# A four-layer graph network on one core: the last layer's order kept in SBUF, its first tile prepared inside the third layer

## The chip, the cores and the metric

The kernel runs on one core of one Trainium2 chip. A core has a matrix engine (PE, with its weight loads shown apart as PEld), VectorE (DVE), ScalarE (ACT), GpSimd (POOL) and a queue engine for transfers (SP). The metric is device time in microseconds (us) of one execution. Engines run their instructions in the order in which they were built into the program, and wait for one another by semaphores.

## The reference, cut to what matters

Eight batches of 2048 nodes with 64 features pass through four layers, each of the form `x = x + layer(relu(layernorm(x)), adj)`. The third and the fourth layer matter here. The third does three message steps with the adjacency matrix, and the fourth is a graph attention:

```python
def _L2_gnn_ref(causal_vars, adj_matrix, W1, b1, W2, b2):   # third layer
    for _ in range(MAX_STEPS):            # 3
        effects = einsum('nm,bmd->bnd', adj_matrix, v)
        h = concatenate([v, effects], axis=-1)
        h = relu(einsum('bnk,dk->bnd', h, W1) + b1)
        v = einsum('bnk,dk->bnd', h, W2) + b2

def _L3_gnn_ref(x, adj, weight, a, bias): # fourth layer
    adj = adj.at[diag_indices(N)].set(1.0)
    h = einsum('bni,io->bno', x, weight)
    e_src = h @ a[:D, 0]
    e_dst = h @ a[D:, 0]
    e = leaky_relu(e_src[:, :, None] + e_dst[:, None, :], negative_slope=0.2)
    e = adj[None, :, :] * e
    attention = softmax(e, axis=-1)
    return einsum('bij,bjd->bid', attention, h) + bias
```

Where adj is 0 the score is 0, not minus infinity, so every node still gives its share with weight exp(0 - maximum). The sum over all nodes of h is therefore used as a base, and only the neighbours' terms differ from it.

## The kernel before, in words

A flag computed at the start picks a short path for sparse graphs; it is the one that runs. The nodes are ordered by the number of their neighbours and cut into 16 tiles of 128. The first tile has the nodes with the most neighbours. For tiles 1 to 15 the kernel makes lists of neighbours, with fixed lengths (`NEAR`: 20, 14, 12, 10, ... 3). The first tile is treated densely.

**The lists** are made by `neighbours` (line 1506) inside the third layer's first steps. It ranks the nodes, writes the order to a small DRAM buffer (`order3`), and then, for tiles 1 to 15, gathers 128 rows of adj at a time with an indirect transfer on POOL (line 1530) into one of two row buffers in slot q4, masks them and takes eight column numbers at a time with VectorE's maximum instruction.

**The third layer** (`layer2`, line 1431) runs three steps of `adj_product`. A step goes over four chunks of 512 nodes. A chunk takes 16 adjacency tiles; ScalarE casts each (line 325), and PE does eight products of 128x128 by 128x512 per tile (line 166). Between two chunks PE makes the messages of the next step, and VectorE adds a bias to them (line 1453). A hook called after every adjacency tile (`after`, line 1461) advances the making of the lists. In the third step each finished chunk goes through `Scores.chunk`: layer norm, projection with the fourth layer's weights, and a store of 528 values per node (features and two sets of scores) to the DRAM tensor `f_rows` (lines 1982 and 1983). There `sq` and `hn` are two buffers in slot q3, and `total`, the sum over all nodes, lies in the first quarter of `sq`.

**The fourth layer** is `layer3_near` (line 1562) with the class `Near` (line 1998). Two generators are interleaved:

- `first_tile` (line 2143) loads the order back from DRAM (line 2022), gathers the first tile's adj rows (line 2149), sets the diagonal and counts (line 2156), transposes them with PE in four groups (line 2164) and copies each group to SBUF (line 2165). It fetches its own feature rows (`mine`), computes a bound on the scores (`highest`) and spreads two vectors of scores over all partitions (lines 2185 and 2186). Then, for each of 16 node tiles, ScalarE does 16 exponentials (lines 2201 and 2202), VectorE a maximum and a mask (lines 2205 and 2206), and PE one product for `plain` and eight for `first`. Each node tile has four stops at which the other generator may go on.
- `others` (line 2080) treats the list tiles in the order `TILES = [15, 13, 11, 1, 10, 2, 9, 3, 8, 4, 7, 5, 6, 12, 14]` (line 2002). `block` (line 2064) gathers one feature row per node and list place: 1 + NEAR[t] indirect transfers of 128 rows each (line 2048), put by POOL into a ring of 36 places. VectorE makes the weights (lines 2093 to 2110) and the products (lines 2119 and 2138), and PE adds them up in `acc` with the identity. The result of a tile goes back to DRAM by another indirect transfer (`put_back`, line 2059). Tiles 15, 13, 11 and 1 fill the ring's 36 places exactly; tile 10 starts over at place 0.

`layer3_near` first takes one step of each, then twelve steps of `first_tile`, and then alternates. After both, `result` loads the rows back and adds them to x. The instructions of each engine are then arranged by a scheduler, so their order is not simply that of the code; tiles in named slots (q0 to q5) are shared by stages, and a write waits for the last reader of its place.

Of the kernel before, what the change touches and what calls it, by code (L numbers as in the profile page):

```python
# [7 lines left out]
F = mybir.dt.float32  # L8
# [3 lines left out]
I32 = mybir.dt.int32  # L12
# [115 lines left out]
class Kernel:  # L128
# [8 lines left out]
    def __init__(self, tc, ctx, a):  # L137
        self.tc, self.nc, self.a = tc, tc.nc, a
        self.flip = 0
        self.short = False  # L140
        self.consts = ctx.enter_context(tc.tile_pool(reuse_waits="tile", name="consts", bufs=1))

        dram = ctx.enter_context(tc.tile_pool(reuse_waits="tile", name="dram", bufs=1, space=bass.MemoryType.DRAM))
        self.xs = [
            [a["xT"][:, :, c * CW : (c + 1) * CW].rearrange("q p n -> p q n") for c in range(NC)]
        ]


        self.h_rows = dram.tile([N, ROW], F, name="h_rows")
        self.g_rows = dram.tile([N, NB * D], F, name="g_rows")  # L150
        self.order3 = dram.tile([P, 2, NT], I32, name="order3")
# [1279 lines left out]
    def layer2(self, slots, k2):  # L1431
# [4 lines left out]
        with (  # L1436
# [19 lines left out]
            if self.short:  # L1456
                near = self.neighbours(k, lambda: ps2.tile([P, CW], F, name="p2"), slots)
            last = Scores(self, slots, k, w, ps2) if self.short else None
            turn = [0]

            def after(ch, m, at):
                turn[0] += 1
                if turn[0] % 2:
                    next(near, None)

            for step in range(3):
                if step == 2:
# [3 lines left out]
                if step > 0:  # L1471
                    for t in range(NT):
                        self.split(u_n, t, u(t))

                def first(ch, out, step=step):
                    s = slice(ch * CW, (ch + 1) * CW)
# [29 lines left out]
    def neighbours(self, k, bank, slots):  # L1506
# [1 line left out]


        nc = self.nc  # L1510
        order = k.tile([P, 2, NT], I32, name="order")
        w = Parts(slots.tile([P, 2 * N], F, name="sort", tag="q4"))
        rank = self.ranks(w, bank, 1, NEAR[1])
        yield
        self.by_rank(w, bank, rank, order)
        nc.sync.dma_start(self.order3, order)
        yield
        own = k.tile([P, NT], F, name="own1")
        nc.vector.tensor_scalar(own, order[:, 1], 1.0, None, op0=OP.add)
        rows = slots.tile([P, 2, N], F, name="near_rows", tag="q4")  # L1520
        line = slots.tile([P, 2, N], F, name="line", tag="q5")
# [6 lines left out]
        for t in range(1, NT):  # L1528
# [33 lines left out]
    def layer3_near(self, slots):  # L1562

        tc = self.tc
        with (
            tc.tile_pool(reuse_waits="tile", name="att", bufs=1) as w,  # L1570
            tc.tile_pool(reuse_waits="tile", name="att_ps", bufs=1, space=PSUM) as ps,
        ):
            near = Near(self, slots, w, ps)
            first = near.first_tile()
            others = near.others()
            next(first)
            next(others)
# [346 lines left out]
class Scores:  # L1924
# [73 lines left out]
class Near:  # L1998
# [5 lines left out]
    def __init__(self, kern, slots, w, ps):  # L2004
        self.kern, self.nc, self.w, self.ps = kern, kern.nc, w, ps
        nc = self.nc
        *_, self.y, self.total, self.rows = kern.last_slots(slots)
        self.turn = 0
        x = slots.tile([P, 2, NP, CW], F, name="x_end", tag="q2")
        more = w.tile([P, 2, NP, CW], F, name="x_more")  # L2010
        self.x = [x[:, 0], x[:, 1], more[:, 0], more[:, 1]]
        two = slots.tile([P, 2, N], F, name="first_row", tag="q0")
        self.row, self.whole = two[:, 0], two[:, 1].bitcast(I32)
# [129 lines left out]
    def first_tile(self):  # L2143

        nc, w, ps, kern = self.nc, self.w, self.ps, self.kern
        ident = kern.ident

        row, whole, at, on_all = self.row, self.whole, self.first_at, self.on_all
        nc.gpsimd.indirect_dma_start(
            row, None, kern.a["adj"], bass.IndirectOffsetOnAxis(ap=self.order[:, 1, :1], axis=0)  # L2150
        )
        nc.gpsimd.iota(whole, pattern=[[1, N]], base=0, channel_multiplier=0)  # L2152
        own = w.tile([P, 1], F, name="own")
        nc.vector.tensor_copy(own, self.order[:, 1, :1])
        few = w.tile([P, 1], F, name="few")
        nc.vector.scalar_tensor_tensor(
            row, whole, own, row, op0=OP.is_equal, op1=OP.max, accum_out=few
        )
        nc.vector.tensor_scalar(few, few, -1.0, float(N), op0=OP.mult, op1=OP.add)
        for g in range(NT // 4):  # L2160
            pt = ps.tile([P, 4, P], F, name="pt", bufs=2)
            for i in range(4):
                c = 4 * g + i
                nc.tensor.transpose(pt[:, i], row[:, c * P : (c + 1) * P], ident)
            nc.scalar.copy(at[:, 4 * g : 4 * g + 4], pt)
# [85 lines left out]
def kernel(tc, a):  # L2251
    with ExitStack() as ctx:
        kern = Kernel(tc, ctx, a)
        with (
# [4 lines left out]

            kern.scores = flags.tile([P, NT, 2 * NB], F, name="scores")  # L2260
            kern.near = flags.tile([P, FIRST[NT]], F, name="near")
            with tc.tile_pool(reuse_waits="tile", name="check", bufs=1) as slots.pool:
                flag = kern.start(flags, slots)
            long = tc.nc.values_load(flag, min_val=0, max_val=1)
# [86 lines left out]
```

## Time and profile before

| | us |
|---|---|
| median of 3 runs | 2163.15 |
| lowest and highest | 2158.54, 2169.57 |
| the profiled execution | 2161.53 |
| its span | 2159.8 |
| PE busy | 1945.0 (90%) |
| DVE busy | 1133.9 (53%) |
| ACT busy | 712.2 (33%) |
| POOL busy | 706.0 (33%) |

The span runs from the first to the last instruction of the profiled execution, and what lies around it makes up the rest of its own time. The fourth layer's gathers begin at 1883.32 us of the span, the last rows are stored by POOL at 2122.93, and the closing transfers end the span. A share of busy time is an average over stages, so each stage has to be read for itself. In a line of the order in time the columns are start, duration, engine, line, operation, output and inputs with their forms, and count; in square brackets stands the idle time before and what ended it. Line numbers are those of the kernel before.

### The profile page before, as it was taken

The numbers are of one execution on the slowest core, as the hardware profiler recorded it, in microseconds if no ns is written. First come the engines' busy times: TensorE is split into PE (matmuls) and PEld (weight loads), VectorE is DVE, ScalarE is ACT, GpSimd is POOL, SyncE is SP. The second block draws the span as 40 slices with busy tenths as digits, with TensorE's granted clock in tenths as the row PEclk, the third lists the DMA queues.
The fourth block names the chain that finished last, engine by engine and source line by source line (L and its number), as shares of the span: only waits on it lengthen the run. The fifth ranks groups of instructions, "written<-read, shape, count | busy, mean of one in ns | idle before, by whom it ended". The sixth has DMA issues, their size and how long they took to land. (4 is left out here: it accounts for less than half of the span.)

```text
span 2159.8 us, 21301 instructions
## 1 busy us (share of the span) xinstructions
PE 1945.0 (90%) x7466; PEld 1163.0 (54%) x7466; DVE 1133.9 (53%) x1956; ACT 712.2 (33%) x1343; POOL 706.0 (33%) x595
## 2 busy tenths in 40 slices
PE   5879999978879999999999998899999999669885
PEld 1425766642237774353453543677777666445433
DVE  7877677736661123425434255698703222248774
ACT  6412555534543440020110201324335333248400
POOL 0000467754310005707447166011000000177870
PEclk8868999987769999999999999999999999879997
DMA  8230333441024460050230500556444444375665
GB/s 318 82 109 6 103 104 116 134 166 39 40 80 126 123 175 31 5 151 1 73 83 0 122 1 28 169 176 223 167 125 129 135 149 147 132 221 166 177 184 183
DMA packets 108796, 253.64 MB, mean 117 GB/s; under 512 B 20912, under 2 KB 21056, under 8 KB 101376
## 3 DMA queue, kind: packets, MB, share of 16 engines
q1 hardware_dynamic: 89264, 181.45, 27.0%
q0 software_dynamic: 17104, 66.47, 10.1%
q10 hardware_dynamic: 2304, 4.20, 0.5%
q8 instruction: 62, 1.02, 0.2%
q14 instruction: 62, 0.51, 0.1%
HBM read 218.30 MB, written 33.78 MB: 117 GB/s over the span
## 5 line engine op out<-in xcount | busy, mean ns | idle before, releaser
L325 ACT CAST adj<-adj_t 128x512 fp32r<-128x512 f32 x384 | 237.4, 619 | 687.2 <-PE pp L166 354.7
L1408 POOL TENSOR_TENSOR acc<-acc,y 128x512 f32<-128x512 f32 x224 | 277.2, 1269 | 449.2 <-DVE y L1403 449.2
L166 PE MATMUL pp<-adj,hi 128*128 128x512 f32 x1280 | 365.6, 405 | 0.1
L166 PE MATMUL pk<-q,w 128*128 128x512 f32 (+1 forms) x1024 | 358.2, 611 | 4.3 <-ACT q L1376 3.0
L166 PE MATMUL pp<-adj,lo 128*128 128x512 f32 x1280 | 358.7, 400 | 0.0
L166 PEld LDWEIGHTS pp<-adj,hi 128*128 128x128 f32 x1280 | 242.1, 191 | 72.4 <-issue 16.0
L166 PEld LDWEIGHTS pp<-adj,lo 128*128 128x128 f32 x1280 | 244.0, 191 | 56.5
L166 PEld LDWEIGHTS pk<-q,w 128*128 128x128 f32 (+1 forms) x1024 | 136.5, 188 | 214.1 <-issue 167.3
L1403 DVE SCALAR_TENSOR_TENSOR y<-pk,bias,q 128x512 f32<-128x512 f32 x224 | 157.7, 746 | 142.0 <-PE pk L166 135.7
L166 PE MATMUL acc<-q,ident 128*128 128x512 f32 x416 | 202.9, 614 | 26.4 <-DVE q L2138 16.5
L2048 POOL DMA_INDIRECT ring<-f_rows,near x121 | 139.7, 1154 | 67.0 <-issue 28.0
L166 PEld LDWEIGHTS acc<-q,ident 128*128 128x128 f32 x416 | 76.7, 194 | 102.4 <-issue 47.2
L2152 POOL IOTA q<- 128x2048 int32 x1 | 1.8, 1834 | 316.5 <-PE p L166 316.5
L166 PE MATMUL pp<-adj,x_ind_hi 128*128 128x512 f32 x256 | 94.7, 486 | 2.2 <-DVE q L738 1.9
L1840 POOL TENSOR_TENSOR q<-q,beta 128x512 f32<-128x512 f32 x57 | 67.9, 1193 | 54.6 <-DVE beta L1816 30.8
L1403 DVE SCALAR_TENSOR_TENSOR acc<-pk,bias,q 128x512 f32<-128x512 f32 x32 | 22.6, 747 | 119.9 <-PE pk L166 119.9
L166 PE MATMUL bank<-std,from_rows 32*128 32x512 f32 x128 | 46.7, 894 | 41.9 <-DVE std L273 33.8
L2119 DVE TENSOR_TENSOR q<-ring,e 128x1024 f32<-128x1024 f32 x58 | 70.1, 1219 | 8.9 <-PE acc L166 8.8
L166 PE MATMUL pp<-adj,x_ind_lo 128*128 128x512 f32 x256 | 71.7, 399 | 0.0
L1530 POOL DMA_INDIRECT q<-in_adj_dram,order x15 | 19.0, 1270 | 160.3 <-DVE top L1544 133.5
L166 PEld LDWEIGHTS pp<-adj,x_ind_hi 128*128 128x128 f32 x256 | 48.5, 189 | 38.9 <-issue 23.7
L1495 DVE SCALAR_TENSOR_TENSOR q<-p,cols,q 128x512 f32<-128x512 f32 x16 | 12.0, 751 | 108.4 <-PE p L166 107.5
(411 smaller groups left out, 2768.4 us busy)
## 6 DMA issues: line engine op xcount, KB each, us to landing
adj_t<-in_adjT_dram SPq DMA_DIRECT2D x128, 512.0 KB, 4.0
adj_t<-in_adjT_dram SPq DMA_DIRECT2D x128, 256.0 KB, 3.3
rows<-in_adj_dram SPq DMA_DIRECT2D x16, 1024.0 KB, 5.6
q<-x SPq DMA_DIRECT2D x10, 1024.0 KB, 4.9
x<-q SPq DMA_DIRECT2D x9, 1024.0 KB, 3.9
q<-in_embT_dram SPq DMA_DIRECT2D x8, 1024.0 KB, 11.5
x_ch<-in_xT_dram SPq DMA_DIRECT2D x4, 1024.0 KB, 6.3
h_rows<-q SPq DMA_DIRECT2D x16, 256.0 KB, 3.6
```

Source lines behind the costliest of these rows:

```text
L166: self.nc.tensor.matmul(out, lhsT, rhs, start=start, stop=stop)
L325: nc.scalar.copy(moving, at[:, i])
L1403: nc.vector.scalar_tensor_tensor(y, pks[b, half], bias[:, b : b + 1], emb[:, b], op0=OP.add, op1=OP.mult,)
L1408: nc.gpsimd.tensor_add(acc, acc, y)
L1495: nc.vector.scalar_tensor_tensor(x[:, q], p2, self.col("b2"), x[:, q], op0=OP.add, op1=OP.add)
L1530: nc.gpsimd.indirect_dma_start(row, None, self.a["adj"], bass.IndirectOffsetOnAxis(ap=order[:, 1, t : t + 1], axis=0),)
L1840: self.nc.gpsimd.tensor_tensor(x, x, by.unsqueeze(2).to_broadcast([P, NB, D]), op=OP.mult)
L2048: self.nc.gpsimd.indirect_dma_start(to, None, self.kern.f_rows[:], bass.IndirectOffsetOnAxis(ap=index, axis=0))
L2119: nc.vector.tensor_tensor(y.rearrange("n i (b f) -> n i b f", b=NB), block[:, i : i + 2, : NB * D].rearrange("n i (b f) -> n i b f", b=NB) ...
L2152: nc.gpsimd.iota(whole, pattern=[[1, N]], base=0, channel_multiplier=0)
```

## The change

- The order stays in an SBUF tile (`kern.order`) that lives through the third and fourth layers; its store to DRAM and its load are gone.
- A new generator, `first_rows`, gathers the first tile's adj rows, sets the diagonal, counts, transposes and copies them. It is advanced by the hook of the third layer's third step, one part per adjacency tile. It reuses the row buffer and the line of numbers of `neighbours`, and writes the turned rows into the half of slot q3 that belonged to `hn`. The iota and the copy of the own number in the fourth layer are gone.
- `hn` now lies in the place of `sq`, so `total` lies in `hn`. The ring of products (`y`) moves from the old `hn` to slot q1, where the turned rows had been.
- In `first_tile`, `mine` is fetched ahead of the first stop, so it comes ahead of the lists' first gathers. Twenty-four steps of `first_tile` instead of twelve are taken before the two generators alternate.

```diff
@@ layer2: @@
+            ahead = iter(())
             turn = [0]

             def after(ch, m, at):
                 turn[0] += 1
                 if turn[0] % 2:
                     next(near, None)
+                next(ahead, None)
...
+                if step == 2 and self.short:
+                    ahead = self.first_rows(slots, lambda: ps2.tile([P, CW], F, name="p2"))
@@ neighbours: @@
-        order = k.tile([P, 2, NT], I32, name="order")
+        order = self.order
...
-        nc.sync.dma_start(self.order3, order)
         yield
-        own = k.tile([P, NT], F, name="own1")
+        own = self.own_next = k.tile([P, NT], F, name="own1")
@@ new: @@
+    def first_rows(self, slots, bank):
+        nc = self.nc
+        row = slots.tile([P, 2, N], F, name="near_rows", tag="q4")[:, 0]
+        line = slots.tile([P, 2, N], F, name="line", tag="q5")[:, 0]
+        *_, at, _ = self.last_slots(slots)
+        nc.gpsimd.indirect_dma_start(
+            row, None, self.a["adj"], bass.IndirectOffsetOnAxis(ap=self.order[:, 1, :1], axis=0)
+        )
+        yield
+        few = self.few
+        nc.vector.scalar_tensor_tensor(
+            row, line, self.own_next[:, :1], row, op0=OP.is_equal, op1=OP.max, accum_out=few
+        )
+        nc.vector.tensor_scalar(few, few, -1.0, float(N), op0=OP.mult, op1=OP.add)
+        yield
+        for g in range(NT // 4):
+            pt = bank()
+            for i in range(4):
+                c = 4 * g + i
+                nc.tensor.transpose(
+                    pt[:, i * P : (i + 1) * P], row[:, c * P : (c + 1) * P], self.ident
+                )
+            nc.scalar.copy(at[:, 4 * g : 4 * g + 4].rearrange("p t n -> p (t n)"), pt)
+            yield
@@ last_slots: @@
-        return one[:, 0], one[:, 1], two[:, 0], two[:, 1], two[:, 0, 0], rows
+        at = two[:, 1].rearrange("p q n -> p (q n)").rearrange("p (t n) -> p t n", t=NT)
+        return one[:, 0], one[:, 1], two[:, 0], two[:, 0, 0], at, rows
@@ layer3_near: @@
-            for _ in range(12):
+            for _ in range(24):
                 next(first)
@@ Scores: @@
-        self.x, self.xr, self.sq, self.hn, self.total, self.rows = kern.last_slots(slots)
+        self.x, self.xr, self.sq, self.total, _, self.rows = kern.last_slots(slots)
+        self.hn = self.sq
@@ Near: @@
-        *_, self.y, self.total, self.rows = kern.last_slots(slots)
+        *_, self.total, self.first_at, self.rows = kern.last_slots(slots)
...
-        two = slots.tile([P, 2, N], F, name="first_at", tag="q1")
-        self.first_at = two[:, 0].rearrange("p (t n) -> p t n", t=NT)
+        two = slots.tile([P, 2, N], F, name="scaled", tag="q1")
+        self.y = two[:, 0].rearrange("p (j n) -> p j n", j=4)
...
-        self.order = w.tile([P, 2, NT], I32, name="order")
-        nc.sync.dma_start(self.order, kern.order3)
+        self.order = kern.order
@@ first_tile: @@
-        row, whole, at, on_all = self.row, self.whole, self.first_at, self.on_all
-        nc.gpsimd.indirect_dma_start(
-            row, None, kern.a["adj"], bass.IndirectOffsetOnAxis(ap=self.order[:, 1, :1], axis=0)
-        )
-        nc.gpsimd.iota(whole, pattern=[[1, N]], base=0, channel_multiplier=0)
...
-        yield
+        at, on_all, few = self.first_at, self.on_all, kern.few
         mine = w.tile([P, WIDE], F, name="mine")
         self.fetch(mine, self.order[:, 1, :1])
+        yield
```

More of the change, by code (lines that the diff above doesn't have):

```diff
@@ L150, in __init__ @@
         self.g_rows = dram.tile([N, NB * D], F, name="g_rows")
-        self.order3 = dram.tile([P, 2, NT], I32, name="order3")
         self.f_rows = dram.tile([N, WIDE], F, name="f_rows")
@@ L2011, in __init__ @@
         self.x = [x[:, 0], x[:, 1], more[:, 0], more[:, 1]]
-        two = slots.tile([P, 2, N], F, name="first_row", tag="q0")
-        self.row, self.whole = two[:, 0], two[:, 1].bitcast(I32)
         self.m = slots.tile([P, 4, NB, P], F, name="m", tag="q0")
         self.att = Halves(slots, "att", ("q0", "q1"), True)
-        two = slots.tile([P, 2, N], F, name="first_at", tag="q1")
-        self.first_at = two[:, 0].rearrange("p (t n) -> p t n", t=NT)
+        two = slots.tile([P, 2, N], F, name="scaled", tag="q1")
+        self.y = two[:, 0].rearrange("p (j n) -> p j n", j=4)
         self.on_all = two[:, 1].rearrange("p (i b n) -> p i b n", i=2, b=NB)
-        self.order = w.tile([P, 2, NT], I32, name="order")
-        nc.sync.dma_start(self.order, kern.order3)
+        self.order = kern.order
         self.near = w.tile([P, FIRST[NT]], I32, name="near")
@@ L2146, in first_tile @@
         ident = kern.ident
-        row, whole, at, on_all = self.row, self.whole, self.first_at, self.on_all
-        nc.gpsimd.indirect_dma_start(
-            row, None, kern.a["adj"], bass.IndirectOffsetOnAxis(ap=self.order[:, 1, :1], axis=0)
-        )
-        nc.gpsimd.iota(whole, pattern=[[1, N]], base=0, channel_multiplier=0)
[L2153 to L2165, printed above, removed]
-        yield
+        at, on_all, few = self.first_at, self.on_all, kern.few
         mine = w.tile([P, WIDE], F, name="mine")
         self.fetch(mine, self.order[:, 1, :1])
+        yield
         es = mine[:, NB * D + NB :]
@@ L2261 @@
             kern.near = flags.tile([P, FIRST[NT]], F, name="near")
+            kern.order = flags.tile([P, 2, NT], I32, name="order3")
+            kern.few = flags.tile([P, 1], F, name="few")
             with tc.tile_pool(reuse_waits="tile", name="check", bufs=1) as slots.pool:
```

## The prediction

> **What bounds the kernel now.** I read the page first: its chain of work that ended last covers only the closing transfers (1% of the span), so it says nothing about the stages that the change touches. Then the stage table (busy time of PE, PEld, DVE, ACT, POOL with instruction counts, granted clock, DMA share, GB/s), then the order in time of each engine.
>
> ```profile
> L2048 POOL DMA_INDIRECT ring<-f_rows,near x121 | 139.7, 1154 | 67.0 <-issue 28.0
> ...
> 1667.00:1850.00 183.00, 180.42 (x747) 127.54 (x747) 44.39 (x89) 62.94 (x109) 0.00 (x0) 0.98 0.41 130
> ...
> 1883.30:1939.00 55.70, 33.59 (x129) 19.96 (x129) 22.20 (x53) 25.20 (x79) 43.18 (x42) 0.78 0.79 242
> 1939.00:2010.00 71.00, 67.71 (x251) 38.67 (x252) 62.81 (x93) 51.23 (x166) 54.15 (x44) 0.94 0.60 170
> 2010.00:2072.60 62.60, 51.25 (x175) 27.45 (x173) 44.67 (x84) 17.35 (x54) 49.56 (x43) 0.92 0.65 182
> 2072.60:2103.50 30.90, 24.21 (x48) 10.01 (x49) 23.67 (x53) 1.85 (x8) 24.68 (x21) 0.83 0.63 183
> ```
>
> Layer 2's last step (1667 to 1850) is PE: 180.4 of 183 us. What is added to PE there is paid. In the last layer the POOL queue sets the pace. Each gather costs 0.95 us and 0.30 us between two, 1.25 us, and POOL takes 42, 44, 43 and 21 of them in the four stretches with hardly a break. Its own order in time:
>
> ```profile
> 1883.32 0.95 POOL L2048 DMA_INDIRECT ring<-f_rows,near  x1 [26.98 <-DMA order<-order]
> 1884.58 0.94 POOL L2149 DMA_INDIRECT q<-in_adj_dram,order  x1 [0.30 <-issue]
> ...
> 1893.33 1.89 POOL L2048 DMA_INDIRECT ring<-f_rows,near  x1 [0.30 <-issue]
> ...
> 1951.86 1.76 POOL L2048 DMA_INDIRECT ring<-f_rows,near  x1 [3.76 <-DVE den L2109]
> ...
> 2072.66 0.94 POOL L2048 DMA_INDIRECT ring<-f_rows,order  x1 [0.30 <-issue]
> ```
>
> From 1883.32 to 2072.66 there is one real wait, 3.76 us at 1951.86: a ring slot of tile 11 isn't read yet, because VectorE stood 13.5 us at tile 1's block. The rest of the excess is slow gathers: of 129 up to 2072.66, 44 take over 1.02 us, and together they are 25.9 us above 0.946 us each. VectorE and PE:
>
> ```profile
> 1555.38 1.36 DVE L1453 TENSOR_TENSOR q<-pn,later 128x512 f32<-128x512 f32 x2 [1.29 <-PE pn L166]
> ...
> 1939.10 0.33 DVE L2093 TENSOR_TENSOR e<-ring 128x168 f32<-128x168 f32 x1 [13.52 <-DMA att_rows<-o,order]
> ...
> 2076.30 0.24 DVE L2093 TENSOR_TENSOR e<-ring 128x80 f32<-128x80 f32 x1 [8.31 <-DMA ring<-f_rows,order]
> ...
> 1905.89 2.89 PE L166 MATMUL pt<-ident,ex 128*128 128x128 f32 x24
> ...
> 2077.70 13.62 PE L166 MATMUL acc<-q,ident 128*128 128x512 f32 x24 [7.69 <-DVE q L2138]
> ```
>
> At 2076.30 VectorE gets tile 5's block (128x80). All of tile 7's products stand behind that instruction, so PE starts cold at 2077.70 and is then the bound: tiles 7, 5, 6, 12 and 14 need 10+11+10+7+6 = 44 products, some 88 records, up to 2121.9. So two numbers set the end: when tile 5's block lands (A, POOL's pace), and PE's run after it (45.6 us). From there to the end it is 37.9 us of transfers, which the change leaves alone.
>
> **What the Trainium skill says.** "SBUF — State Buffer", section "SBUF: two separate sides", says that VectorE and GpSimd share a port pair as an exclusive lock and that descriptor generation on GpSimd is locked out meanwhile. The trace agrees: while VectorE is idle (1926 to 1939) every gather is 0.95 to 1.00 us, and at full VectorE load many take 1.5 to 2.0. "TensorE: Matmul & The Clock Gate", section "What's actually happening", has PE fall to half clock after an idle window of about 3.4 us; here the granted clock is 0.50 from 1885 to 1895, after PE stopped at 1879.4, and a 512-wide record of two takes about 0.95 us instead of 0.45. "DMA: Bandwidth & Descriptors", section "Anatomy of one DMA — SWDGE (gpsimd) path", gives a fixed 2.0 us plus bytes over 436 GB/s, 2.6 us for 270 KB; the trace says 3.4 to 6.8 us (median 3.9), and I use that.
>
> **The change, part by part.** Where I say new order, I mean the order in which the changed program's instructions stand on each engine, which is fixed when it is built. All times are against the profiled execution, 2161.53 us with a span of 2159.8; it lies 1.62 us below the median of the runs, 2163.15.
>
> 1. The first tile's rows of adj are gathered in layer 2. POOL loses one issue ahead of all lists: -1.25. Their VectorE pass (2.42 us at 1891.99) is also gone from there, and with it the slow gather at 1893.33 (1.89 for 0.95): -0.94. The own-number cast and the iota go; both lay in idle time. In layer 2 the gather can go out once tile 14's buffer is read (1546.97) and takes about 7 us (L1530: 5.4 to 9.8), so it lands near 1554.2; by the new order its VectorE pass stands ahead of the additions that began at 1555.38. It ends near 1556.8, the additions start 1.4 to 1.7 us late, and PE's third group (1556.71), which waits for a bank, about 1.2 us late: +1.2, with 0 and 4 as ends (landing at 5.4 and 9.8 us).
>
> 2. Sixteen transposes of 128x128 move into PE's bound step. The warm row above gives 2.89/24 = 0.12 us each, the cold ones at L2164 0.22: +1.9, ends 1.8 and 3.5. The first four stand in PE's order from the second chunk boundary of layer 2's second step on, near 1592 in the trace, 35 us after their rows are ready. The four ScalarE copies (0.58 each) fit in its idle time there (about 1.25 us per adjacency tile). Without that cover they would cost 2.3.
>
> 3. The order's way through DRAM: SP loses two small transfers. The second was issued at 1880.78, behind the last feature rows (1880.35). The first POOL issue needs those rows anyway, so I take 0, at most -0.5. x_more's two loads go out 0.46 us earlier; nobody waits.
>
> 4. hn takes sq's place: within a chunk the order square, variance, write is already forced, and the next chunk is some 37 us away: 0. The copy of total now waits for one product more; VectorE reaches it one group later in the new order: 0 to 0.3, I take 0.
>
> 5. Twenty-four steps of the first tile ahead of the lists instead of twelve. `mine` becomes POOL's first gather, at 1883.3 instead of 1896.78, and lands near 1888; the sixteen products for `plain` (0.9 us each while PE stays warm), ten of which stand ahead of the small products with ex, keep PE until about 1889.5. So ScalarE's first exponential goes from 1907.6 to about 1892. Its pace is 16 x 0.29 + 0.5 = 5.2 us for one node tile. VectorE's new order puts tile 15's products behind the sixth maximum, tile 13's behind the seventh, tile 11's behind the ninth: by 1892 + 2.3 (four copies) + 1.8 (the second block's small work stands ahead of the first maximum) + 6 x 5.2 that is 1927, then 1932, and 1943 to 1945 for the ninth. POOL reaches the slots to be overwritten at 1883.3 + 37 x 1.25 + about 4 for slow gathers = 1933.5 (tile 15's), four gathers of 1.4 later at 1939 (tile 13's), and four gathers and two writes of about 1.6 later at 1948.7 (tile 11's). The products are read some 3 to 5 us after those maxima, so the waits are nearly even; I put +1.0 for new ones. The old wait of 3.76 goes, as VectorE fills its 13.5 us idle with the first tile's work: -3.46 (3.76 less the usual 0.30). Slow gathers otherwise stay: the same VectorE instructions meet the same POOL.
>
> 6. In the new POOL order the first tile's write stands one block earlier, ahead of tile 5's gathers: +1.3 on A.
>
> So A moves by -1.25 - 0.94 - 3.46 + 1.0 + 1.3 = -3.35. After A the new VectorE order again holds tile 7 behind tile 5's block, but tile 4's products now run just before it. PE idles some 2.6 us instead of 7.69 and probably stays warm: it ran at half clock from 2077.7 to 2084.2, which cost 3.25; I take -2.3, with 0 and -3.6 as ends. Layer 2 adds 3.1. Sum: -3.35 - 2.3 + 3.1 = -2.55, so 2159.0 for the profiled execution and **2160.6** for the median.
>
> **Rivals.** *Within 0.5%, the forecast.* 0.5% of 2163 is 10.8 us, about what a measurement of this kernel can tell from no change; POOL keeps as many issues ahead of A as before (one gather less, one write more).
>
> *Faster by over 0.5%.* The dense stretch (1939 to 2010) gives 71.0/44 = 1.61 us a gather, the first stretch 55.7/42 = 1.33. Twice as many of the first tile's maxima and masks move into a stretch where gathers are cheap. If all 44 went at 1.33, A would gain 12.5 us more: about 2148; with two thirds of it 2152. For it: the cheap stretches are those with VectorE idle. Against: the moved instructions slow gathers wherever they run.
>
> *Slower by over 0.5%: VectorE's fixed order holds the ring.* If the first exponential comes late, every list product behind a maximum is late by as much, POOL stops at slots 0 to 14, and all that follows shifts. It decides from a first exponential at about 1893; each us beyond costs one. Should PE be cold for the ten `plain` products (1.9 us each, as at 1898), it would be 1902: 9 us of waits in place of 1.0, and with late additions in layer 2 (+2.8 more) and a cold PE after A (+2.3) the time is 2173.7, where this case begins. Against: PE was warm until 1879.4 and now continues without a pause.
>
> That the change doesn't take place is excluded: the new order shows the transposes in layer 2.
>
> **How the numbers follow.** Forecast 0.58, faster 0.28, slower 0.14: my figures for slow gathers and the waits of point 5 are the weak ones, and both errors push outwards. The likeliest case alone spans 2154 to 2168 by the ends of points 1, 2, 5 and the warm PE. Eight in ten: 2149 to 2171, which takes in most of the faster rival and the mild part of the slower.
>
> **What would show it.** Right: POOL's first gather near 1886 (1883.3 and layer 2's 3 us) for `mine`; one POOL issue fewer; no wait over 2 us before tile 5; transposes in layer 2 at 0.12 us; the additions near 1557; PE's last run after tile 5 about 42 us. Wrong: waits of POOL on VectorE in its first 70 us, gathers of the dense stretch near 1.35 us, or PE starting the last run cold.

## The result, and the profile after

The changed kernel takes 2171.99 us in the median of 12 runs (2161.01 to 2181.99), the kernel before 2162.28 (2156.99 to 2169.57, 12 runs). The ratio is 1.0040, its 95% interval 1.0022 to 1.0059: slower by about 9 us. A second measurement, below, gave 1.0039 (1.0026 to 1.0052). The prediction was 2160.6 us. It falls short by 11 us and has the wrong sign; the time lies 1 us above its range of 2149 to 2171, though still within the 0.5% that it called no change. The profiled execution of the changed kernel took 2172.84 us, its span is 2171.0.

**Third layer.** The stage table of the changed kernel (busy time of PE, PEld, DVE, ACT, POOL with instruction counts, then granted clock, DMA share, GB/s), for its third layer's last step and the four stretches of the fourth layer:

```profile
1670.00:1856.50 186.50, 183.91 (x760) 129.95 (x759) 44.52 (x89) 64.88 (x113) 0.00 (x0) 0.97 0.39 128
1889.30:1945.00 55.70, 41.85 (x163) 30.94 (x162) 24.17 (x43) 40.18 (x132) 42.38 (x41) 0.69 0.76 230
1945.00:2016.00 71.00, 67.08 (x245) 36.82 (x244) 64.81 (x107) 47.09 (x155) 55.28 (x42) 0.98 0.54 154
2016.00:2081.00 65.00, 47.50 (x122) 22.31 (x122) 39.71 (x83) 3.44 (x13) 51.06 (x46) 0.84 0.68 193
2081.00:2112.00 31.00, 23.85 (x45) 9.52 (x44) 19.16 (x42) 1.03 (x5) 21.79 (x21) 0.83 0.65 192
```

PE's step is 3.5 us longer. ScalarE's work moved forward (40.18 us in the first 55.7 instead of 25.20, and 3.44 in the third stretch instead of 17.35), as the 24 steps ask. POOL got no further for it: 41 and 42 instructions in the first two stretches, where it had 42 and 44.

The groups of costly instructions, POOL's gathers of list rows, and then POOL's order in time (start, duration, then the idle time before it and what ended it):

```profile
L2078 POOL DMA_INDIRECT ring<-f_rows,near x121 | 137.4, 1136 | 40.9 <-issue 27.4
```

```profile
1889.31 0.95 POOL L2078 DMA_INDIRECT mine<-f_rows,order  x1 [338.30 <-DVE mx L2074]
...
1946.24 0.94 POOL L2078 DMA_INDIRECT ring<-f_rows,near  x1 [2.36 <-DVE q L2168]
...
1949.52 1.71 POOL L2078 DMA_INDIRECT ring<-f_rows,near  x1 [0.60 <-DVE q L2149]
...
1958.36 1.78 POOL L2078 DMA_INDIRECT ring<-f_rows,near  x1 [2.00 <-DVE den L2139]
...
2081.07 0.95 POOL L2078 DMA_INDIRECT ring<-f_rows,order  x1 [0.30 <-issue]
```

The wait of 3.76 us, at tile 11's place in the ring, is down to 2.00, and two new ones of 2.36 and 0.60 us stand ahead of it, at tile 13's: VectorE hasn't read the places that POOL wants to fill. Together they are 4.06 us beyond the usual 0.30 each, before 3.46. From POOL's first gather to that at 2081.07, which answers 2072.66 of before, it is 191.76 us instead of 189.34, with 129 issues in both (one gather less, one write more). Of these 2.42 us, 0.6 are waits and 1.8 slow gathers (27.7 us above 0.946 us each, before 25.9). Over the 121 gathers of the line above, those behind it included, the mean is 1.136 us, before 1.154.

VectorE's order in time, first in the third layer and then where it begins the weights of tiles 7, 5 and 6:

```profile
1555.97 2.35 DVE L1568 SCALAR_TENSOR_TENSOR q<-q,own,q 128x2048 f32<-128x2048 f32 x1 [1.12 <-DMA q<-in_adj_dram,order]
...
1558.44 1.28 DVE L1452 TENSOR_TENSOR q<-pn,later 128x512 f32<-128x512 f32 x2
...
2068.19 0.23 DVE L2123 TENSOR_TENSOR e<-ring 128x72 f32<-128x72 f32 x1 [7.55 <-DMA ring<-f_rows,order]
...
2083.67 0.24 DVE L2123 TENSOR_TENSOR e<-ring 128x80 f32<-128x80 f32 x1 [3.12 <-DMA ring<-f_rows,near]
...
2097.80 0.23 DVE L2123 TENSOR_TENSOR e<-ring 128x72 f32<-128x72 f32 x1 [3.30 <-issue]
```

PE in the same places (a group of transposes, then the list products; a product is two records, and a group of records runs over into the next tile by a product or two):

```profile
1682.41 0.60 PE L1577 MATMUL p<-ident,q 128*128 128x128 f32 x4
...
2069.61 13.36 PE L165 MATMUL acc<-q,ident 128*128 128x512 f32 x26 [6.76 <-DVE q L2168]
...
2087.53 9.40 PE L165 MATMUL acc<-q,ident 128*128 128x512 f32 x18 [1.84 <-DVE q L2149]
2098.69 1.13 PE L165 MATMUL acc<-q,ident 128*128 128x512 f32 x2 [1.76 <-DVE q L2168]
2101.78 12.52 PE L165 MATMUL acc<-q,ident 128*128 128x512 f32 x22 [1.96 <-DVE q L2149]
```

VectorE takes up tile 5's block (128x80) 194.36 us after POOL's first gather, before 192.98. PE stands idle for under 2 us at a time there instead of 7.69, but not all of tile 7's products run warm (at the full granted clock), as the prediction had it: 18 records take 9.40 us at a granted clock of 0.85, in the repeat of the change further down 7.99 us at 1.00. It has done them at 2096.9, and tile 5's products stand on VectorE behind its start on tile 6's block (the second 128x72), which comes at 2097.80. Before, VectorE waited 0.63 us for that, and PE still had work. Now VectorE waits 3.30, PE idles twice, and tile 5's 22 records take 12.52 us instead of 9.71.

These waits don't end when the tile's own block is there. By the landing times that the traces give, tile 5's last gather landed at 2079.84 and tile 6's at 2093.60 (before at 2072.60 and 2085.92). All 20 waits of over 0.5 us ahead of these two tiles, in the fourteen profiles of this document, end 0.08 to 0.22 us after the second gather of the next tile has landed, 3.0 to 4.4 us after the tile's own last one. Why VectorE waits for that gather isn't shown. It holds for both kernels, so it doesn't explain their difference.

The last row is stored 11.93 us later (2122.93 to 2134.86). By the two profiles:

| part | change, us |
|---|---|
| end of the third layer's last chunk (1851.70 to 1858.18) | +6.48 |
| from there to POOL's first gather (31.62 to 31.13) | -0.49 |
| from there to VectorE's start on tile 5's block (192.98 to 194.36) | +1.38 |
| from there to the last row stored (46.63 to 51.19) | +4.56 |

Not all of the 6.48 us is the change. It was 1.0 us late already at 1520 (POOL's gather of 1520.73 comes at 1521.74). The table below takes the third layer chunk by chunk, from one ScalarE activation that ends a chunk to the next:

| kernel | chunk of the additions | next two | chunk of the transposes | last step's other three |
|---|---|---|---|---|
| before | 37.21 | 37.21, 37.22 | 37.21 | 50.69, 50.70, 49.09 |
| changed | 38.78 | 37.33, 37.34 | 38.75 | 52.45, 49.23, 50.81 |

Against the plain chunks of the same kernel (37.33), the move costs 1.5 us in one chunk and 1.4 in another. The three last chunks come out at 49.2, 50.7 or 52.5 us in an order that has nothing to do with the edit (the kernels below show it too; the last section says what decides it); that makes 1.6 of the 6.48 us. The plain chunks are themselves 0.12 us longer, some 0.9 over these seven: 37.33 to 37.34 in all eleven kernels of this document that keep the order on chip, 37.21 to 37.22 in the three that don't. What of that edit does it isn't shown. The parts that the change can explain are 2.95 - 0.5 + 1.4 + 4.6 = 8.4 us, a ratio of 1.0039, and 9.3 us with the 0.9. That this meets the measured 1.0040 is in part luck, as 4.6 and 1.4 are figures of one profile each.

### The profile page after: what moved, and what is told of

Its sections match the earlier page's. It is cut to its first block, busy times and chain, and to the rows that moved or that the text cites. A ratio compares the mean times of both kernels' runs of the same rounds, so it can differ in the third digit from the quotient of the medians.

```text
span 2171.0 us, 21293 instructions
## 1 busy us (share of the span) xinstructions
PE 1952.2 (90%) x7466; PEld 1168.4 (54%) x7466; DVE 1133.9 (52%) x1955; ACT 710.5 (33%) x1343; POOL 703.9 (32%) x594
## 5 line engine op out<-in xcount | busy, mean ns | idle before, releaser
L165 PE MATMUL acc<-q,ident 128*128 128x512 f32 x416 | 208.6, 632 | 36.2 <-DVE q L2168 22.4
L2149 DVE TENSOR_TENSOR q<-ring,e 128x1024 f32<-128x1024 f32 x58 | 69.9, 1220 | 14.1 <-PE acc L165 13.7
```

The lines of the kernel that those rows point to most:

```text
L165: self.nc.tensor.matmul(out, lhsT, rhs, start=start, stop=stop)
L2149: nc.vector.tensor_tensor(y.rearrange("n i (b f) -> n i b f", b=NB), block[:, i : i + 2, : NB * D].rearrange("n i (b f) -> n i b f", b=NB) ...
```

## The experiments

The first theory, **steps**: the 24 steps give VectorE's and POOL's work of the fourth layer an order that costs some 6 us. The rival, **move**: the rows made in the third layer cost all of it. Below, "the stretch" is the time from POOL's first gather to the last row stored, 239.6 us before and 245.6 changed, a figure of one profile each. The fourth layer of the changed kernel, as it is, has three profiles in this document and took 241.3, 245.6 and 249.3 us in them, so one pair of stretches that lies some 4 us apart shows nothing by itself.

**One part undone.** The changed kernel with 12 steps:

```diff
-            for _ in range(24):
+            for _ in range(12):
```

> The changed kernel with 12 steps of the first tile ahead of the lists instead of 24; all else stays. Theory 'steps' (the fourth layer's new arrangement costs some 6 us: from POOL's first gather to the last row stored it took 239.6 us before and 245.6 after): this undoes it, so that stretch comes back to 240 us or a little less, and what is left over the kernel before is the third layer's 3.5 us: about 2165 against 2162 and 2172. Theory 'move' (the rows made inside the third layer cost all of it, by the transposes and by what they delay): no change against the changed kernel, about 2172.

Measured: 2165.87 us, ratio to before 1.0012 (0.9996 to 1.0029). The stretch is 239.3 us, and POOL has no wait of over 0.6 us in it. So the number of steps is worth about 6 us by the ratios and by the stretches alike (the ratios' intervals overlap a little), and what is left over before is the size of the move's 3 us.

**The steps alone.** The kernel before with 24 steps:

```diff
-            for _ in range(12):
+            for _ in range(24):
```

> The kernel before with 24 steps of the first tile ahead of the lists instead of 12, and nothing else of the change. Theory 'steps': about 6 us slower than the kernel before, 2168. Theory 'move': the same as before, 2162. A third possibility: with the first tile's rows still gathered behind the first list block, its exponentials start at 1907 and not at 1899, the maxima that stand ahead of tile 15's products come later, and POOL waits for the ring longer than in the changed kernel: 2172 or more.

Measured: 2184.01 us, ratio 1.0086 (1.0060 to 1.0111): the third possibility, and more of it than I had put. The stretch is 258.7 us. POOL's order in time:

```profile
1973.32 1.76 POOL L2048 DMA_INDIRECT ring<-f_rows,near  x1 [18.67 <-DVE den L2109]
```

Here the first exponential starts 22.5 us after POOL's first gather, in the changed kernel 9.5. Thirteen us later at ScalarE are 16 us more of waits at POOL (20.0 instead of 4.1 in all).

**Everything but the move.** The kernel before with the order on chip, `mine` first and 24 steps:

```diff
-        order = k.tile([P, 2, NT], I32, name="order")
+        order = self.order
-        nc.sync.dma_start(self.order3, order)
...
-            for _ in range(12):
+            for _ in range(24):
...
+        mine = w.tile([P, WIDE], F, name="mine")
+        self.fetch(mine, self.order[:, 1, :1])
         nc.gpsimd.indirect_dma_start(
             row, None, kern.a["adj"], bass.IndirectOffsetOnAxis(ap=self.order[:, 1, :1], axis=0)
         )
...
```

> The kernel before with the order kept on chip, mine fetched first and 24 steps, but with the first tile's rows still gathered and turned in the fourth layer. VectorE's order of the fourth layer's list work is then that of the changed kernel; only the third layer is free of the move. Theory 'steps': some 6 us slower than before, about 2168, and the third layer's end at about 1851.7 to 1853 instead of 1858. Theory 'move': as before, 2162. Should the move have been a gain that the steps ate up, it is slower than the changed kernel: over 2172, because the rows' gather (1.25 us on POOL) and the adj pass stand in the fourth layer again.

Measured: 2163.39 us, ratio 0.9998 (0.9978 to 1.0017). The median says "move", the profile "steps": a stretch of 245.8 us with the third layer's chunks at 37.3 throughout. I ran it again with the changed kernel beside it:

> The kernel with all but the move once more, since its runs (ratio 0.9998) and its profile don't agree: in the profile POOL's first gather to the last row stored takes 245.8 us, 6.1 more than before, with the third layer unchanged. Theory 'steps': by the stages 2162.3 + 6.4, a ratio of 1.003. If the ratio is again 1.000, something outside these stages gives 6 us back (the layers ahead of it, or the closing transfers, which took 34.1 us in that profile against 36.9), and the move alone is then what separates the changed kernel from the kernel before.

> The changed kernel again, beside the other kernels of this call on the same chip, as their common measure. By the first measurement a ratio of 1.004. By the stages: third layer 3.0 us more, POOL's first gather 0.5 us earlier after the layer's end, from there to the last row stored 5.9 us more: 8.4 us, 1.0039.

Measured: 2167.90 us, ratio 1.0018 (1.0005 to 1.0031), and 2172.51 us, ratio 1.0039 (1.0026 to 1.0052). Their stretches are 242.2 and 249.3 us. So both theories have part of it: the new order without the move costs 0 to 4 us by the runs, 3 to 6 by the two profiles, and the move adds 4.5 us by the ratios (0.0021), 3 by the chunks. The order kept on chip gives nothing by itself: from the third layer's end to POOL's first gather these two took 31.9 and 31.4 us, before 31.6.

**The price of the transposes.** Each group of four, with its copy, eight times:

```diff
-        for g in range(NT // 4):
+        for g in list(range(NT // 4)) * 8:
```

> The changed kernel with each group of four transposes and its copy on ScalarE made eight times: 112 more transposes and 28 more copies in the third layer's last step, same output. It prices the move's part on PE. By the changed kernel's trace a group takes PE some 0.36 us: 28 x 0.36 = 10 us slower than the changed kernel, about 2182. By the prediction's 0.12 us a transpose: 28 x 0.48 = 13.4 us, about 2185. If ScalarE's copies (0.58 us) held up its casts and so PE, each group would cost up to 1.06 us: 30 us, about 2202.

Measured: ratio 1.0104 (1.0069 to 1.0139), 0.0064 above the changed kernel: 13.8 us for 28 groups, 0.49 each (with an uncertainty of some 0.3). In PE's order in time an adjacency tile with a group takes 2.31 us (from 1685.19 to 1687.50), one without 1.88, so a group 0.43. The stretch of this kernel, whose fourth layer is that of the changed kernel, is 241.3 us, with waits of 2.0 us at POOL instead of 4.1:

```profile
1685.19 1.18 PE L165 MATMUL pp<-adj,hi 128*128 128x512 f32 x4
1686.21 1.10 PE L165 MATMUL pp<-adj,lo 128*128 128x512 f32 x4
1687.14 0.60 PE L1577 MATMUL p<-ident,q 128*128 128x128 f32 x4
1687.50 1.17 PE L165 MATMUL pp<-adj,hi 128*128 128x512 f32 x4
```

ScalarE's casts still wait for PE there and not the other way round, so its copies are hidden:

```profile
1692.52 0.58 ACT L1580 COPY q<-p 128x512 f32<-128x512 f32 x1
1694.31 0.62 ACT L324 CAST adj<-adj_t 128x512 fp32r<-128x512 f32 x1 [1.21 <-PE pp L165]
```

**More of the steps.** If VectorE's order holds the ring, 36 steps must hold it longer.

```diff
-            for _ in range(24):
+            for _ in range(36):
```

> The changed kernel with 36 steps of the first tile ahead of the lists instead of 24. VectorE then has eight or nine pairs of a maximum and a mask ahead of the second list tile's products, where the changed kernel has six and the one with 12 steps three; ScalarE makes one pair's exponentials in 5.2 us. POOL comes to these ring places 50 us after its start. Theory 'order holds the ring': the products come some 3 x 5.2 us later, and POOL's waits grow from 4.1 us to about 18; from its first gather to the last row stored about 258 us, the whole about 2184. Theory 'contention' (slow gathers beside VectorE's work, not its order): no more waits, the stretch as in the changed kernel, 246 us and 2172.

Measured: 2190.22 us, ratio 1.0103 (1.0076 to 1.0130), a stretch of 260.5 us. POOL's order in time:

```profile
1959.09 1.76 POOL L2078 DMA_INDIRECT ring<-f_rows,order  x1 [18.85 <-DVE den L2139]
```

With 12, 24 and 36 steps the waits are 0.3, 4.1 and 18.6 us. The excess of slow gathers hardly moves (32.3, 29.6 and 32.8 us up to the last gather), so it isn't contention that the steps change. That is the mechanism of the prediction's slower rival: more of it makes more of the waits.

**The tail.** A second suspect is what follows tile 5's block. In this kernel VectorE may begin a tile's weights only when the products of the tile before are made, for the last five tiles:

```diff
-            e = w.tile([P, NEAR[1] + 1, NB], F, name="e", bufs=2)[:, :n]
+            at_e = 0 if place > 9 else place % 2
+            e = w.tile([P, NEAR[1] + 1, NB], F, name=f"e{at_e}", bufs=1)[:, :n]
```

> The changed kernel, but the weights e of tiles 7, 5, 6, 12 and 14 share one buffer, so that VectorE can begin a tile's weights only when the products of the tile before are made. Nothing ahead of tile 7's products moves. In the changed kernel tile 7's products stand behind tile 5's block and tile 5's behind tile 6's, which lands at 2097.80; PE then starts cold and needs 37.1 us to the last row stored. Theory 'tail order' (that standing behind the next block costs the changed kernel its tail): PE goes on from tile 4's products at 2069.6 with 13.4 + 44 x 0.885 us of products and some 3 us of gaps; from POOL's first gather to the last row stored 245.6 us become about 236, the whole about 10 us less, 2162. Theory 'pace' (POOL's gathers alone set the end, whatever the order behind them): 245 and 2172 stay.

> The same edit on the kernel before. Theory 'tail order': tile 7's products no longer wait for tile 5's block (8.31 us of idle at 2076.30); the last gather at 2102.49 lands some 4 us later, and behind it come 3 us of weights and 5.4 us of products: the last row stored at about 2115 instead of 2122.93, 7 us less, about 2156. Theory 'pace': no change, 2163. It would also say whether the kernel before has the same weakness, hidden only because its PE was late.

> The changed kernel with both edits: 12 steps of the first tile ahead of the lists, and one buffer for the weights of the last five tiles. With 12 steps alone, POOL's first gather to the last row stored took 239.3 us, of which 35.1 from tile 6's block on. Theory 'tail order': some 7 us less, 232, and the whole about 2158, 4 us under the kernel before although the third layer still pays its 3 us for the move. Theory 'pace': 239 and 2166 stay.

Measured, as ratios to before and as stretches (with the time from VectorE's start on tile 6's block to the last row stored):

| kernel | tail as it was | last five tiles with one buffer |
|---|---|---|
| before | 1; 239.6 (33.5) | 0.9984 (0.9972 to 0.9996); 236.8 (28.4) |
| changed, 24 steps | 1.0040 (1.0022 to 1.0059); 245.6 (37.1) | 1.0009 (0.9997 to 1.0020); 238.3 (27.3) |
| changed, 12 steps | 1.0012 (0.9996 to 1.0029); 239.3 (35.1) | 1.0001 (0.9987 to 1.0015); 233.7 (27.3) |

The edit takes some 0.3% off the changed kernel, 0.16% off the kernel before and 0.1% off the one with 12 steps, the last within the noise. The theory "pace", that the gathers alone set the end, falls. The figures in brackets alone overstate the gain, since with one buffer VectorE comes to tile 6's block later, when more is done; the stretches say it rightly. In the changed kernel the gain in the stretch is 7.2 us where I had put 10: POOL's last gather is 3.4 us later there (220.8 us after its first). PE's order in time with 24 steps and one buffer:

```profile
2063.24 14.30 PE L165 MATMUL acc<-q,ident 128*128 128x512 f32 x28 [6.66 <-DVE q L2169]
2077.75 7.13 PE L165 MATMUL acc<-q,ident 128*128 128x512 f32 x16 [0.20 <-DVE q L2150]
...
2086.91 11.50 PE L165 MATMUL acc<-q,ident 128*128 128x512 f32 x24 [0.63 <-DVE q L2169]
2099.09 9.36 PE L165 MATMUL acc<-q,ident 128*128 128x512 f32 x20 [0.69 <-DVE q L2150]
```

No gap is over 0.7 us from tile 4's first product on. The two cures overlap: either of them takes away most of what the change costs, both together little more. That fits a chain, waits that delay POOL, a block that comes late, a PE that stands idle for it.

**PE kept busy in the gap.** Is it the cold clock that makes tile 5's records long?

```diff
                     kern.mm(acc, kern.ident, y[:, j], start=i + j < 0, stop=i + j == n - 1)
+                    if t == 5 and i < 0:
+                        pt = self.ps.tile([P, 4, P], F, name="pt", bufs=2)
+                        for _ in range(2):
+                            kern.mm(pt.rearrange("n q f -> n (q f)"), kern.ident, y[:, j])
```

> The changed kernel with four more products for PE whose result nobody reads: two behind each of the first two products of tile 5, in the gaps of 1.76 and 1.96 us that PE has there. Theory 'cold': tile 5's other products then run warm, 22 records in about 9.7 us instead of 12.5; from tile 6's block to the last row stored about 34.3 us instead of 37.1, the whole 2.8 us less (0.13%, hardly to be told by the runs' times alone, so the stretch decides). If PE's clock isn't what makes these records long, the stretch stays at 37 us, or grows by up to 3.5 us, should the added products hold up others.

Measured: 2171.62 us, ratio 1.0049 (1.0033 to 1.0065); from VectorE's start on tile 6's block to the last row stored 36.8 us, no gain. PE's order in time:

```profile
2106.97 2.07 PE L165 MATMUL acc<-q,ident 128*128 128x512 f32 x2 [3.03 <-DVE q L2172]
2108.84 3.62 PE L165 MATMUL pt<-q,ident 128*128 128x512 f32 x4
2112.25 10.07 PE L165 MATMUL acc<-q,ident 128*128 128x512 f32 x22
```

The 22 records did fall to 10.07 us. But of the added products the first two had run ahead of the gap, and the second two ran cold themselves (3.62 us for four records) and took the time that was won. As a cure it failed; VectorE waited 6.28 us for tile 6's block in this profile, so the gap was longer than what I filled. The answer came from elsewhere: runs whose fourth layer has VectorE's list work in the very same order, at the end at least. In the repeat of all but the move VectorE waited 0.85 us for tile 6's block. Tile 5's 22 records there, and their time as a line of the stage table:

```profile
2100.31 9.71 PE L165 MATMUL acc<-q,ident 128*128 128x512 f32 x22 [1.49 <-DVE q L2116]
...
2100.31:2110.02 9.71, 9.71 (x22) 4.09 (x22) 8.90 (x19) 0.45 (x2) 6.82 (x6) 1.00 0.61 184
```

In the repeat of the change it waited 6.93:

```profile
2110.69 12.54 PE L165 MATMUL acc<-q,ident 128*128 128x512 f32 x22 [0.85 <-DVE q L2149]
...
2110.69:2123.23 12.54, 12.54 (x22) 5.18 (x22) 8.92 (x19) 0.43 (x2) 5.33 (x6) 0.77 0.42 134
```

All six profiles with this order at the end:

| kernel | VectorE's wait for tile 6, us | granted clock in tile 5's 22 records | the records, us | from VectorE's start on tile 6 on, us |
|---|---|---|---|---|
| all but the move, repeat | 0.85 | 1.00 | 9.71 | 34.3 |
| transposes eight times | 1.94 | 1.00 | 9.71 | 34.2 |
| before with 24 steps | 2.08 | 0.85 | 11.41 | 35.9 |
| changed | 3.30 | 0.77 | 12.52 | 37.1 |
| all but the move | 3.41 | 0.76 | 12.65 | 37.1 |
| changed, repeat | 6.93 | 0.77 | 12.54 | 36.9 |

So the cold clock does make these records long, by up to 2.9 us. The length of the wait alone doesn't set by how much: in two other orders waits of 4.37 (12 steps) and 6.49 us (36 steps) went with 11.41 and 11.14 us. Nor did PE stay warm all the time in the first two rows. Its clock was low while it did tile 7's products there (0.75 in the first, where 20 records took 11.73 us), and was back when tile 5's came.

**The late additions.** One more edit on the kernel with 12 steps and the mended tail: the row buffer is first touched by VectorE after the chunk's last message, which holds the gather back (`late` is that message).

```diff
-    def first_rows(self, slots, bank):
+    def first_rows(self, slots, bank, late):
...
+        nc.vector.tensor_copy(row[:, :1], late[:, :1])
         nc.gpsimd.indirect_dma_start(
             row, None, self.a["adj"], bass.IndirectOffsetOnAxis(ap=self.order[:, 1, :1], axis=0)
         )
```

> The kernel with 12 steps and the tail's order mended, and one more edit: one column of the row buffer is first written by VectorE from the last messages of the chunk, so that the gather of the first tile's rows in the third layer, and the pass over them, come behind the four additions that PE waits for and not ahead of them. Theory 'late additions' (the pass ahead of the additions is half of what the move costs in the third layer: that chunk took 38.8 us against 37.2 to 37.3 in kernels without the move): the chunk comes back to 37.3 us, the other chunk, with the transposes, stays at 38.75. If the 1.5 us come from something else (the gather's traffic, say), it stays at 38.8. The whole: about 2161, 1.5 us less than without this edit.

Measured: 2160.25 us, ratio 0.9982 (0.9970 to 0.9994). The chunk of the additions takes 37.32 us, that of the transposes 38.74. VectorE's order in time:

```profile
1558.84 1.36 DVE L1452 TENSOR_TENSOR q<-pn,later 128x512 f32<-128x512 f32 x2 [1.24 <-PE pn L165]
...
1562.88 0.15 DVE L1563 COPY q<-q 128x1 f32<-128x1 f32 x1
1569.28 2.35 DVE L1569 SCALAR_TENSOR_TENSOR q<-q,own,q 128x2048 f32<-128x2048 f32 x1 [6.25 <-DMA q<-in_adj_dram,order]
```

The additions wait for PE again and not PE for them. The chunk shows these 1.5 us, the runs by themselves don't: the kernel without this last edit measured 1.0001 (0.9987 to 1.0015), and its stretch was shorter (233.7 us, here 237.0). In the eight other kernels with the move that chunk took 38.5 to 39.8 us, in the five without it 37.2 to 37.3. This version and the kernel before with the mended tail (0.9984) are both faster than the kernel before, by about 0.2%, and can't be told apart.

## Why the prediction was wrong

**Right.** The move in the third layer: +3.1 predicted, 1.5 + 1.4 = 2.95 measured. The additions come late as said (+1.2 predicted). The transposes cost a bit less than 1.9 because their first group, at 1592.78 behind the end of a chunk, makes that chunk no longer (37.33); a group measures 0.43 to 0.49 us against 4 x 0.12. The copies are hidden. The way of the order through DRAM gives nothing. POOL's first gather is `mine`, and the rows' gather is gone ahead of the lists. That hn's new place costs nothing was not tried by itself. What the prediction had at nothing and isn't, is the 0.12 us on every chunk of the kernels that keep the order on chip.

**Wrong, point 5, the new waits (+1.0, measured 4.1).** The places are right: tile 13's products stand behind the seventh maximum and tile 11's behind the ninth, and POOL waits at both. The sizes are not. The first exponential came 9.5 us after POOL's first gather, where I had 8.7, but that isn't what made the waits: in the repeat of the change it came after 8.75, and they were 3.8 us. The maxima began 5.66 us apart (1905.82 to 1934.13 for six), not 5.2, the seventh 51.3 us after POOL's first gather instead of 48.7, and VectorE stood 2.50 us at tile 13's products for PE. So I found the mechanism and called it nearly even. The gain of 3.46 for the old wait was paid back in full.

**Wrong, point 1, slow gathers (-0.94).** The slow gather beside the rows' pass is gone, but up to the gather that answers 2072.66 the excess of all slow ones rose from 25.9 to 27.7 us, one profile against one. Moving VectorE's work didn't take it out of POOL's way: all gathers and writes of over 1.35 us (34 before, 37 after, up to 2125) lie beside a VectorE pass over two tensors, TENSOR_TENSOR but for one. The section that the prediction names for this has the lock for VectorE's two-port modes, and for passes with two SBUF inputs only against a GpSimd operation that reads SBUF; by the traces the gathers are slow beside the latter. With the waits this turned -3.35 for A into +1.4.

**Wrong, the term after A (-2.3, measured +4.6).** This is the largest miss and the step that failed, one that I had not questioned: "PE is then the bound" after tile 5's block. It was so before only because tile 7's products began late and cold: they filled the time until VectorE came to tile 6's block. With PE early, that is the bound, since tile 5's products stand behind it in VectorE's order just as tile 7's stand behind the start on tile 5's. It came 13.1 us after the start on tile 5's block before and 14.1 after the change, so a faster PE could win nothing. Then it lost its clock, which is 2.8 of the 4.6 us (12.52 us for 9.71) and, by the table above, not the same from profile to profile. The kernel with one buffer for the last tiles shows what this order costs: its stretch is 7.2 us shorter. Nor was A what I took it for: by the landing times above, tile 5's own block had been there for 3.7 us at 2076.30, and VectorE's wait ended with a gather of tile 6.

**The rivals.** The slower one, "VectorE's fixed order holds the ring", is what happened in part. Of the tail behind it that rival had named the cold PE alone, and not that VectorE's order is the bound there. The faster one is refuted: gathers of the dense stretch take 71.0/42 = 1.69 us, not 1.33.

What stays open is the share of each. The new order without the move measured 0.9998 and 1.0018, and its stretch 245.8 and 242.2 us in two profiles. The move's 0.0021 has an interval that includes its 3 us but doesn't show them.

## What to carry to other kernels

When a wait ahead of a fixed order is taken away, ask what each engine will wait for next in that order, one buffer further on, and not only whether it is faster: here every tile's products stood behind VectorE's wait for later data, and one buffer less for the last five tiles, which only changes when VectorE may begin a tile, was worth 0.1 to 0.3%. Moving work of an idle engine forward is not free if a ring is read behind it; count how many of its instructions stand ahead of the first read, times their pace, against the time at which the ring is full. A move out of the last stage into a stage bound by PE pays PE's price (here 0.43 to 0.49 us for each group of four transposes), and its VectorE pass should be placed by a dependency, behind the instructions that PE waits for.

## What the runs showed of the hardware

The same order of instructions has tails from 34.2 to 37.1 us, by how much of tile 5's work meets a lowered clock. "TensorE: Matmul & The Clock Gate" in the Trainium skill, section "What's actually happening", says that the window which decides this runs freely, so that it depends on where in it the work lands. The traces agree: in all fourteen the granted clock is 1.00 or 0.50, and it changes only at times that lie whole multiples of 3.41 us apart, in the changed kernel's tail at 2066.5, 2073.3, 2087.0, 2090.4, 2100.6 and 2107.5.

The same decides the last step's chunks. The changed kernel's three, as lines of the stage table:

```profile
1705.69:1758.14 52.45, 51.60 (x201) 35.42 (x200) 13.10 (x27) 17.68 (x31) 0.00 (x0) 0.93 0.43 140
1758.14:1807.37 49.23, 48.36 (x201) 33.13 (x200) 13.01 (x27) 17.67 (x31) 0.00 (x0) 1.00 0.45 152
1807.37:1858.18 50.81, 49.94 (x201) 34.38 (x200) 13.10 (x27) 15.82 (x29) 0.00 (x0) 0.97 0.29 98
```

Chunks of 49.1 to 49.2 us have no stretch at half clock, those of 50.7 to 50.9 one of 3.41 us, and those of 52.4 to 52.5 two. It is so in all 40 such chunks of the fourteen profiles that have no added transposes, with or without the change. One such stretch costs 1.6 us here: six score products at 1727.03 took 1.69 us in the chunk of 52.45, and six at 1778.59 took 0.94 in that of 49.23.

The gather of the first tile's rows in the third layer took POOL 2.79 us to issue (at 1548.22, while VectorE made a pass of 128x2048 that began at 1547.87), where the one before it took 0.94. It cost nothing here, since nothing stood behind it.
